# A decoder layer in three stages: staggered stage starts, and a layer norm whose reciprocal root is found by Newton steps on GpSimd

## The chip, the cores and the metric

The kernel runs on one core of a Trainium2 chip. The core has five engines that work side by side, each through its own queue in order: TensorE (PE in the profile, with its weight loads as PEld) for matrix products, VectorE (DVE) for elementwise work, reductions and scans, ScalarE (ACT) for functions taken from tables and for copies, GpSimd (POOL) for further elementwise work, and SyncE (SP), which here issues DMA transfers. Engines wait for each other by semaphores. The metric is the time of one execution on the device in microseconds (us), less being better.

## What is computed

The input `x` has 16 sequences of 256 positions and 256 channels, `ctx_1024` the same shape. Everything is in 32-bit floats. The layer is three blocks, each added to its input and then normalised:

```
x = layernorm(x + mixer(x))
x = layernorm(x + cross_attention(x, ctx, ctx))
x = layernorm(x + feed_forward(x))
layernorm(x) = (x - mean(x)) / sqrt(var(x) + 1e-5)
```

- **mixer**: a projection `x @ in_proj_w`, a causal convolution over four positions, and per head a weight `p_w` (an exponential of a score, times a time weight). Values are multiplied by `theta`; `cos` and `sin` of the products, times a polynomial of the value and `p_w`, are summed cumulatively over positions and divided by the cumulative sum of `p_w`. The result is normalised by its root mean square, projected with `W_re` and `W_im`, gated with a Silu and projected out.
- **cross attention** by autocorrelation: query, key and value projections, a Fourier transform over positions, the correlation of query and key, the five best shifts per head, a softmax over them, and the sum of the values rolled by those shifts.
- **feed-forward**: two branches of eight experts. Each is `(x V) * cumsum(x W)`, weighted by a softmax router with a Gelu layer, and projected back with `U`; the sum goes through `W_O`.

## The kernel before

Sequences are handled in pairs, `NP = 8` pairs in all. Three Python generators emit the instructions of a pair:

- `mixer(p)` (line 407) issues the loads of `x` for pair p+1 (`load_x`, line 86, on SyncE's DMA queue), emits `body(p)` (line 237) and then `front(p + 1)` (line 179). `front` transposes x (L187), projects it (L196, L213), convolves (`convolve`, L172 and L174), and makes the weights, their cumulative sum `den` and the gated products `g` (L222 to L224); its last act is Silu on two tiles (L229). `body` runs four rounds: four DMA transfers spread rows over partitions (`spread`, L235), ScalarE makes the angles and takes sines (L253 to L259), VectorE multiplies and scans (L261, L262, and L117 in `cumsums`), ScalarE squares (L267, L268), TensorE projects and sums (L272, L277). Then comes a square root over `sv` (L289), the output projection (L304) and the layer norm with tag "ml".
- `attention(p)` (line 565) loads the context, transforms and projects (`spectra`: L432, L438, L442, L461, L472, L478), picks the shifts (`choose`, L492 to L526), rolls (`rolled`: L535, L552, L562), and ends with the layer norm "al". `spectra` adds an output bias to `x` on GpSimd (L453).
- `feed_forward(p)` (line 580) transposes x (L589), scans it (L591), runs the router (L599, Gelu at L601, L602, softmax from L611 to L624, L629, L634), broadcasts the router's weights by DMA (L645), runs the two wide products for each of eight blocks (L649, L653) with VectorE's multiplications (L650, L654), then the output product (L663, L664), the layer norm "fl", and writes the result out (L670).

Each generator yields after a piece of work, with a number that stands for its size. `run` (line 313) takes several generators with their totals (70 for a mixer, 45 for an attention, 77 for a feed-forward) and always advances the one that has done the smallest share of its total. So the instructions of the three streams are traced in proportion to each other.

The main loop (line 674) has nine steps. Step p runs `mixer(p)`, `attention(p - 1)` and `feed_forward(p - 2)` together, each from its start to its end; the streams of step p+1 begin to be traced when all of step p are traced. Before it stand `front(0)` and `mixer(0)` with the folding of weights (`fold_weights`, line 365).

The order of tracing is not the order on the engines: a planner takes it as a priority, and places instructions by its own idea of when their inputs and buffers will be ready. It also gives out the buffers. Those that matter here: nine buffers for `x` (half a pair each), `xT` and `fxT` one each, two each for `sn`, `cs` and `ge`, three for `wb`, eight for `e`, and in PSUM two banks for the mixer (`m_bank`) and four that attention and feed-forward share (`f_bank`).

`layernorm` (line 153) works on four tiles of 128x256 at once. VectorE takes mean and variance of each (L158, L159); ScalarE takes the square root of the four variances (L161, with EPS as bias); VectorE makes the reciprocal (L162) and minus mean times reciprocal (L163); ScalarE scales and shifts each tile (L165). ScalarE holds one set of function tables at a time; where the next function is in another set, an ACT_TABLE_LOAD stands before it in the profile, under the line of that function.

Of the kernel before, what the change touches and what calls it, by code (L numbers as in the profile page):

```python
# [11 lines left out]
F32 = mybir.dt.float32  # L12
BF16 = mybir.dt.bfloat16
U32 = mybir.dt.uint32
AF = mybir.ActivationFunctionType
ALU = mybir.AluOpType
# [3 lines left out]
P = 128  # L20
# [9 lines left out]
EPS = 1e-5  # L30
NP = B // 2
HG = 16
MAGIC = 12582912.0
FAR = 3.0e38
TWO_PI = 2.0 * math.pi
TWO_PI_DOWN = float(np.nextafter(np.float32(TWO_PI), np.float32(0.0)))

# [13 lines left out]
def decoder_kernel(ctx: ExitStack, tc: tile.TileContext, a: dict, out: bass.AP):  # L51
    nc = tc.nc
    V, S, G, T = nc.vector, nc.scalar, nc.gpsimd, nc.tensor
# [18 lines left out]
    def m_bank():  # L72
        return m_ps.tile([P, 512], F32, name="mps", tag="mps")
# [4 lines left out]
    def split(ps, n=2):  # L78
        return ps.rearrange("p (c d) -> p c d", c=n)
# [6 lines left out]
    def load_x(b):  # L86
        xs[b] = mx.tile([P, 2, D], F32, name="x", tag="x", bufs=9)
        nc.sync.dma_start(out=xs[b], in_=a["x"][b].rearrange("(c p) d -> p c d", p=P))
# [19 lines left out]
    b_magic, b_half_pi, b_eps = bias_c[:, 0:1], bias_c[:, 1:2], bias_c[:, 2:3]  # L108
# [6 lines left out]
    def cumsums(dst, src):  # L115

        V.tensor_tensor_scan(dst, again[:, : dst.shape[1]], src, 0.0, ALU.mult, ALU.add)  # L117
# [29 lines left out]

    V.tensor_scalar(tcol, tcol, 1.0 / TWO_PI, None, ALU.mult)
    for i in range(2):
# [3 lines left out]
    def layernorm(pool, tag, tiles):  # L153
        n = len(tiles)
        st = pool.tile([P, n, 6], F32, name="ln_st", tag=tag + "st")
        mv = pool.tile([P, n, 2], F32, name="ln_mv", tag=tag + "mv")
        for i, t in enumerate(tiles):
            V.bn_stats(st[:, i, :], t)  # L158
            V.bn_aggr(mv[:, i, :], st[:, i, :])  # L159
        sd = pool.tile([P, 3, n], F32, name="ln_sd", tag=tag + "sd")  # L160
        S.activation(sd[:, 0, :], mv[:, :, 1], AF.Sqrt, bias=b_eps)  # L161
        V.reciprocal(sd[:, 1, :], sd[:, 0, :])  # L162
        V.scalar_tensor_tensor(sd[:, 2, :], mv[:, :, 0], -1.0, sd[:, 1, :], ALU.mult, ALU.mult)  # L163
        for i, t in enumerate(tiles):
            S.activation(t, t, AF.Identity, scale=sd[:, 1, i : i + 1], bias=sd[:, 2, i : i + 1])  # L165


    def convolve(pool, tag, ps, ci, bufs):

        zc = pool.tile([P] + list(ps.shape[1:]), F32, name=tag, tag=tag, bufs=bufs)  # L170
        cw = pv[:, C_CW + 4 * ci : C_CW + 4 * ci + 4]
        S.activation(zc, ps, AF.Identity, bias=pv[:, C_CB + ci : C_CB + ci + 1], scale=cw[:, 3:4])  # L172
        for s in (1, 2, 3):
            V.scalar_tensor_tensor(  # L174
                zc[..., s:], ps[..., : L - s], cw[:, 3 - s : 4 - s], zc[..., s:], ALU.mult, ALU.add
            )
        return zc

    def front(p, made):

        xT = mx.tile([P, 2, 2, L], F32, name="xT", tag="xT")
        for j in range(2):
            ps = m_bank()
            for db in range(2):
                for c in range(2):
                    lo = db * L + c * P
                    T.transpose(ps[:, lo : lo + P], xs[2 * p + j][:, c, db * P : (db + 1) * P], ident)  # L187
            S.copy(xT[:, :, j, :], split(ps))


        ps = m_bank()
        for c in range(2):
            for par in range(2):
                for j in range(2):
                    q = 32 * (2 * par + j)
                    T.matmul(ps[q : q + 32, :L], w_sc[:, c, par, :], xT[:, c, j, :], start=c == 0, stop=c == 1)  # L196
        yield 3
        sc = convolve(mx, "sc", ps[:, :L], 4, 1)
        V.tensor_scalar(sc, sc, pv[:, C_SCALE : C_SCALE + 1], 20.0, ALU.mult, ALU.min)
        V.tensor_scalar(sc, sc, -20.0, None, ALU.max)  # L200
        pw = sc
        S.activation(pw, sc, AF.Exp)
        V.tensor_tensor(pw, pw, tw, ALU.mult)
        den = mx.tile([P, L], F32, name="den", tag="den", bufs=2)
        cumsums(den, pw)
        V.tensor_scalar(den, den, 1e-4, None, ALU.max)
        yield 3

        zcs, gs = [], []
        for m in range(4):  # L210
            ps = m_bank()
            for c in range(2):
                T.matmul(ps, w_in[:, c, m * P : (m + 1) * P], xT[:, c, :, :], start=c == 0, stop=c == 1)  # L213
            zcs.append(convolve(mx, "zc", split(ps), m, 6))
            if m < 2:
                g = mx.tile([P, 2, L], F32, name="g", tag="g", bufs=3)
                ps = m_bank()
                for j in range(2):
                    T.matmul(
                        ps[:, j * L : (j + 1) * L], sel_h[:, j, m * P : (m + 1) * P], pw, start=True, stop=True  # L220
                    )
                S.activation(g, zcs[m], AF.Identity, bias=dw[:, 1:2], scale=dw[:, 3:4])  # L222
                G.tensor_tensor(g, g, zcs[m], ALU.mult)
                V.scalar_tensor_tensor(g, g, dw[:, 0:1], split(ps), ALU.add, ALU.mult)  # L224
                gs.append(g)
            if m < 3:
                yield 4
        for m in (2, 3):
            S.activation(zcs[m], zcs[m], AF.Silu)  # L229
        made[p] = zcs, gs, den  # L230
        yield 4
# [5 lines left out]
    def body(p, made):  # L237
        zcs, gs, den = made.pop(p)
        ss = y_ps.tile([P, L], F32, name="ss", tag="ss")
        for m in range(2):  # L240
            y = y_ps.tile([P, 512], F32, name="y", tag="y")
            for h in range(2):
# [15 lines left out]
                S.activation(cs, cs, AF.Abs)  # L258
                S.activation(cs, cs, AF.Sin, bias=b_half_pi, scale=-TWO_PI)  # L259
                yield 3  # L260
# [38 lines left out]
        for j in range(2):  # L299
# [8 lines left out]
            V.tensor_tensor(x, x, split(ps), ALU.add)  # L308
            tiles += [x[:, 0, :], x[:, 1, :]]
        layernorm(mx, "ml", tiles)  # L310
        yield 4

    def run(*streams):


        left = [[0.0, n, total, gen] for n, (gen, total) in enumerate(streams)]
        while left:
            at = min(left, key=lambda s: (s[0] / s[2], s[1]))
            try:
                at[0] += next(at[3])  # L320
            except StopIteration:
                left.remove(at)

    made = {}
    run((front(0, made), 22))


    f_dft = load("f_dft", [P, 2, 2, 64], eng=G)
# [24 lines left out]
    m5 = const.tile([2 * NH, 8], F32, name="m5", tag="m5")  # L353
    V.memset(m5, FAR)

# [51 lines left out]
    def mixer(p):  # L407
        if 2 * p + 2 < B:
            for b in (2 * p + 2, 2 * p + 3):
                if xs[b] is None:  # L410
                    load_x(b)
        yield from body(p, made)
        if p + 1 < NP:
            yield from front(p + 1, made)

    with tc.tile_pool(name="fold", bufs=1) as fold:
        for b in range(2, 4):
            load_x(b)
        run((mixer(0), 70))
        fold_weights(fold)  # L420

    at = ctx.enter_context(tc.tile_pool(name="at", bufs=1))
# [22 lines left out]
    def load_ctx(b):  # L445
        ct = at.tile([P, 2, D], F32, name="ct", tag="ct", bufs=2)
        nc.sync.dma_start(out=ct, in_=a["ctx"][b].rearrange("(c p) d -> p c d", p=P))
        return ct
# [37 lines left out]
    def choose(prod, wfs):  # L486
# [14 lines left out]
        rest = at.tile([NHP, L], F32, name="rest", tag="rest")  # L501
        V.match_replace(rest, m5, corr, -FAR)
        V.tensor_scalar(m8, m8, top[:, 0:1], None, ALU.add)
# [5 lines left out]
        V.reciprocal(top[:, 4:5], top[:, 3:4])  # L509
        V.scalar_tensor_tensor(corr, rest, -FAR, corr, ALU.is_equal, ALU.mult)  # L510
        S.activation(corr, corr, AF.Identity, scale=top[:, 4:5])
# [53 lines left out]
    def attention(p):  # L565
        prod = at.tile([P, 4, 2 * NH], F32, name="prod", tag="prod", bufs=2)
        pair = (2 * p, 2 * p + 1)
        cts = [load_ctx(b) for b in pair]
        vfs, wfs = [], []
        for b, ct in zip(pair, cts):  # L570
            yield from spectra(b, ct, prod, vfs)
        yield from choose(prod, wfs)
        for b, vf in zip(pair, vfs):
            rolled(b, vf, wfs[0])
            yield 5
        layernorm(at, "al", [xs[b][:, c, :] for b in pair for c in range(2)])
        yield 3
# [93 lines left out]
        yield 3  # L671


    for p in range(1, NP + 2):
        streams = []
        if p < NP:
            streams.append((mixer(p), 70))
        if p - 1 < NP:
            streams.append((attention(p - 1), 45))
        if p >= 2:  # L680
            streams.append((feed_forward(p - 2), 77))
        run(*streams)

# [124 lines left out]
```

## Time and profile before

| What | Value |
|---|---|
| median of 3 runs | 1166.14 us (1166.03 to 1169.14) |
| the profiled execution | 1166.22 us |
| its span on the core | 1164.5 us |
| granted TensorE clock, mean | 0.925 of full speed |
| PE busy | 982.4 us |
| DVE busy | 722.9 us |
| ACT busy | 593.0 us |
| ACT_TABLE_LOAD on ACT | 97, of 1283 ns each |
| POOL busy | 166.3 us |
| layer norms | 24, of four tiles each |

The profile is one execution, taken by the hardware profiler. The span reaches from the first to the last instruction of the core; busy time is the time in which an engine executes instructions. A busy PE is not a PE at its peak: ends of matmuls are modelled, and the granted clock varies. Rows of the form "L163 DVE ..." name a source line, engine, operation and tile. In the table of stretches each row gives start and end, length, then for each engine busy us and number of instructions, then the granted clock, the share of DMA time and GB/s.

### The profile page before, as it was taken

The numbers are of one execution on the slowest core, as the hardware profiler recorded it, in microseconds if no ns is written. First come the engines' busy times: TensorE is split into PE (matmuls) and PEld (weight loads), VectorE is DVE, ScalarE is ACT, GpSimd is POOL, SyncE is SP. The second block draws the span as 40 slices with busy tenths as digits, with TensorE's granted clock in tenths as the row PEclk, the third lists the DMA queues.
The fourth block names the chain that finished last, engine by engine and source line by source line (L and its number), as shares of the span: only waits on it lengthen the run. The fifth ranks groups of instructions, "written<-read, shape, count | busy, mean of one in ns | idle before, by whom it ended". The sixth has DMA issues, their size and how long they took to land.

```text
span 1164.5 us, 10813 instructions
## 1 busy us (share of the span) xinstructions
PE 982.4 (84%) x3820; PEld 542.4 (47%) x3820; DVE 722.9 (62%) x1173; ACT 593.0 (51%) x831; POOL 166.3 (14%) x163
## 2 busy tenths in 40 slices
PE   5878858789987899779987799779988799699787
PEld 2335426234652457334662457334662358246345
DVE  5766877676685666765775766766775754234132
ACT  2865664863288425972279425972279522311310
POOL 4002102020111111210111111211111111101000
PEclk9988869889998899889999899889999899999889
DMA  9612312163043413333033513334032510040050
GB/s 322 158 37 73 81 37 46 36 109 46 2 91 80 82 19 73 82 67 51 1 82 77 95 19 73 73 58 60 1 82 55 89 20 1 18 64 9 19 72 19
DMA packets 45510, 72.04 MB, mean 62 GB/s; under 512 B 4448, under 2 KB 18320, under 8 KB 45456
## 3 DMA queue, kind: packets, MB, share of 16 engines
q1 hardware_dynamic: 44240, 68.04, 29.2%
q0 software_dynamic: 1216, 3.31, 0.9%
q8 instruction: 30, 0.49, 0.2%
q14 instruction: 24, 0.20, 0.0%
HBM read 16.81 MB, written 4.19 MB: 18 GB/s over the span
## 4 chain that ended last, share of the span: by engine, by line
PE 58%; ACT 15%; DVE 14%; DMA 5%; issue 3%; POOL 3%; SPq 1%; POOLq 0%; ACTq 0%; DVEq 0%
PE fps L649 10%; PE fps L653 9%; PE fps L663 5%; PE fps L461 4%; PE fps L599 4%; DMA sn<-zc 3%; PE y L272 3%; DVE cs L117 3%; PE fps L602 2%; PE mps L304 2%; ACT x L165 2%; PE fps L552 2%; PE fps L472 2%; PE mps L213 2%; DVE sn L117 2%
## 5 line engine op out<-in xcount | busy, mean ns | idle before, releaser
L649 PE MATMUL fps<-fcT,w_c 128*128 128x512 f32 x256 | 137.4, 656 | 0.0
L653 PE MATMUL fps<-fxT,w_v 128*128 128x512 f32 x256 | 124.5, 609 | 0.0
L663 PE MATMUL fps<-u_o,e 128*128 128x256 f32 x512 | 116.9, 379 | 0.0
L663 PEld LDWEIGHTS fps<-u_o,e 128*128 128x128 f32 x512 | 97.3, 190 | 15.8 <-issue 2.9
L599 PE MATMUL fps<-fxT,w_h 128*128 128x512 f32 x128 | 75.1, 726 | 15.6 <-ACT fxT L590 15.6
L653 PEld LDWEIGHTS fps<-fxT,w_v 128*128 128x128 f32 x256 | 50.3, 199 | 67.4 <-issue 57.1
L650 DVE TENSOR_TENSOR e<-wb,fps 128x512 f32<-128x512 f32 x64 | 43.7, 683 | 61.0 <-DMA wb<-fwT 31.4
L174 DVE SCALAR_TENSOR_TENSOR zc<-mps,pv,zc 128x510 f32<-128x510 f32 (+2 forms) x96 | 70.7, 738 | 16.1 <-ACT zc L172 15.1
L117 DVE TENSOR_TENSOR_SCAN sn<-again,sn 128x1024 f32<-128x1024 bf16 x32 | 78.0, 2438 | 0.5
L117 DVE TENSOR_TENSOR_SCAN cs<-again,cs 128x1024 f32<-128x1024 bf16 x32 | 77.3, 2415 | 0.4
L213 PE MATMUL mps<-xT,in_proj_w 128*128 128x512 f32 x128 | 65.1, 626 | 13.9 <-DVE g L224 10.2
L261 DVE TENSOR_TENSOR sn<-sn,ge 128x1024 f32<-128x1024 f32 x32 | 43.4, 1356 | 43.7 <-ACT sn L257 36.4
L649 PEld LDWEIGHTS fps<-fcT,w_c 128*128 128x128 f32 x256 | 49.4, 208 | 42.8 <-issue 39.3
L253 ACT ACTIVATE sn<-sn,theta_col 128x512 f32<-128x512 f32 x64 | 45.5, 714 | 46.5 <-DMA sn<-zc 46.0
L654 DVE TENSOR_TENSOR e<-e,fps 128x512 f32<-128x512 f32 x64 | 43.4, 677 | 33.7 <-PE fps L653 32.8
L461 PE MATMUL fps<-Wkv,spec 128*128 128x512 f32 x128 | 61.8, 615 | 2.8 <-ACT spec L442 2.8
L478 POOL TENSOR_TENSOR pp<-qf,kf 128x512 f32<-128x512 f32 x16 | 22.3, 1397 | 278.9 <-ACT qf L476 278.9
L599 PEld LDWEIGHTS fps<-fxT,w_h 128*128 128x128 f32 x128 | 27.3, 231 | 64.6 <-issue 45.3
L272 PE MATMUL y<-cs,w_ri 128*32 128x512 f32 x128 | 38.9, 689 | 20.4 <-DVE cs L117 17.3
L602 PE MATMUL fps<-h,w2t 128*32 128x512 f32 x64 | 34.2, 690 | 25.4 <-ACT h L601 25.4
L165 ACT ACTIVATE x<-x,ln_sd 128x256 f32<-128x256 f32 x96 | 50.1, 588 | 6.6 <-DVE ln_sd L163 6.6
L268 ACT ACTIVATE sq<-cs 128x1024 f32<-128x1024 f32 x32 | 33.7, 1054 | 35.4 <-PE ss L277 29.2
(231 smaller groups left out, 1823.7 us busy)
## 6 DMA issues: line engine op xcount, KB each, us to landing
sn<-zc SPq DMA_DIRECT2D x64, 256.0 KB, 4.7
ge<-g SPq DMA_DIRECT2D x64, 256.0 KB, 4.7
wb<-fwT SPq DMA_DIRECT2D x64, 256.0 KB, 4.4
x<-in_x SPq DMA_DIRECT2D x16, 256.0 KB, 3.1
ct<-in_ctx SPq DMA_DIRECT2D x16, 256.0 KB, 2.7
out<-x SPq DMA_DIRECT2D x16, 256.0 KB, 3.0
in_proj_w<-in_in_proj_w SPq DMA_DIRECT2D x1, 512.0 KB, 6.0
V_fwd<-in_V_fwd SPq DMA_DIRECT2D x1, 512.0 KB, 10.9
```

The costliest lines, as they stand in the source:

```text
L117: V.tensor_tensor_scan(dst, again[:, : dst.shape[1]], src, 0.0, ALU.mult, ALU.add)
L165: S.activation(t, t, AF.Identity, scale=sd[:, 1, i : i + 1], bias=sd[:, 2, i : i + 1])
L174: V.scalar_tensor_tensor(zc[..., s:], ps[..., : L - s], cw[:, 3 - s : 4 - s], zc[..., s:], ALU.mult, ALU.add)
L213: T.matmul(ps, w_in[:, c, m * P : (m + 1) * P], xT[:, c, :, :], start=c == 0, stop=c == 1)
L253: S.activation(sn[:, i, :], sn[:, i, :], AF.Identity, scale=tcol[:, cb : cb + 1])
L272: T.matmul(y[q : q + 32, :], w_ri[:, n, :], part[:, i, :], start=n == 0, stop=n == 1)
L461: T.matmul(ps, cf[:, c, f * P : (f + 1) * P], wkv[:, c, :], start=c == 0, stop=c == 1)
L599: T.matmul(ps, w_h[:, c, br, rb * P : (rb + 1) * P], xT[:, c, :, :], start=c == 0, stop=c == 1)
L602: T.matmul(pl[32 * br : 32 * br + 32, :], w2t[:, rb, :], h, start=rb == 0, stop=rb == 1)
L649: T.matmul(pc, w_c[:, c, br, cut], cT[:, c, :, :], start=c == 0, stop=c == 1)
L653: T.matmul(pv_, w_v[:, c, br, cut], xT[:, c, :, :], start=c == 0, stop=c == 1)
L663: T.matmul(o, es[i][:, cut], u_o[:, i, :], start=i == 0, stop=False)
```

## The change

There are two parts. First, the nine separate runs become one. Every stream gets a start and a length on a common scale of steps: `mixer(p)` starts at p and lasts 1; `attention(p)` starts at p + 1.2 and lasts 1; `feed_forward(p)` starts at p + 2.6 and lasts 1. `run` always advances the stream whose place on that scale is the earliest. Before, the starts in that scale were p, p + 1 and p + 2.

Second, `layernorm` no longer takes a square root on ScalarE. VectorE adds EPS to the variances and makes a first guess of the reciprocal root from the bits of the number (a shift, and a subtraction from a constant); GpSimd improves it in three Newton steps of four operations each, and makes minus mean times the result in two more. All work on 128x4 elements. ScalarE's scaling of the tiles is as before.

```diff
--- before.py
+++ after.py
@@ -32,6 +32,9 @@
 HG = 16
 MAGIC = 12582912.0
 FAR = 3.0e38
+
+A_AT, A_LEN = 0.2, 1.0
+F_AT, F_LEN = 1.6, 1.0
 TWO_PI = 2.0 * math.pi
 TWO_PI_DOWN = float(np.nextafter(np.float32(TWO_PI), np.float32(0.0)))
 
@@ -157,12 +160,21 @@
         for i, t in enumerate(tiles):
             V.bn_stats(st[:, i, :], t)
             V.bn_aggr(mv[:, i, :], st[:, i, :])
-        sd = pool.tile([P, 3, n], F32, name="ln_sd", tag=tag + "sd")
-        S.activation(sd[:, 0, :], mv[:, :, 1], AF.Sqrt, bias=b_eps)
-        V.reciprocal(sd[:, 1, :], sd[:, 0, :])
-        V.scalar_tensor_tensor(sd[:, 2, :], mv[:, :, 0], -1.0, sd[:, 1, :], ALU.mult, ALU.mult)
+
+        rs = pool.tile([P, 5, n], F32, name="ln_rs", tag=tag + "rs")
+        var, y, t, nb, half = (rs[:, i, :] for i in range(5))
+        V.tensor_scalar(var, mv[:, :, 1], EPS, None, ALU.add)
+        V.tensor_scalar(half.bitcast(U32), var.bitcast(U32), 1, None, ALU.logical_shift_right)
+        V.tensor_scalar(y.bitcast(U32), half.bitcast(U32), -1.0, float(0x5F3759DF), ALU.mult, ALU.add)
+        for _ in range(3):
+            G.tensor_tensor(t, y, y, ALU.mult)
+            G.tensor_tensor(t, t, var, ALU.mult)
+            G.tensor_scalar(t, t, -0.5, 1.5, ALU.mult, ALU.add)
+            G.tensor_tensor(y, y, t, ALU.mult)
+        G.tensor_tensor(nb, mv[:, :, 0], y, ALU.mult)
+        G.tensor_scalar(nb, nb, -1.0, None, ALU.mult)
         for i, t in enumerate(tiles):
-            S.activation(t, t, AF.Identity, scale=sd[:, 1, i : i + 1], bias=sd[:, 2, i : i + 1])
+            S.activation(t, t, AF.Identity, scale=y[:, i : i + 1], bias=nb[:, i : i + 1])
 
 
     def convolve(pool, tag, ps, ci, bufs):
@@ -313,16 +325,16 @@
     def run(*streams):
 
 
-        left = [[0.0, n, total, gen] for n, (gen, total) in enumerate(streams)]
+        left = [[start, length / total, gen] for start, length, total, gen in streams]
         while left:
-            at = min(left, key=lambda s: (s[0] / s[2], s[1]))
+            at = min(left, key=lambda s: s[0])
             try:
-                at[0] += next(at[3])
+                at[0] += at[1] * next(at[2])
             except StopIteration:
                 left.remove(at)
 
     made = {}
-    run((front(0, made), 22))
+    run((0, 1, 22, front(0, made)))
 
 
     f_dft = load("f_dft", [P, 2, 2, 64], eng=G)
@@ -416,7 +428,7 @@
     with tc.tile_pool(name="fold", bufs=1) as fold:
         for b in range(2, 4):
             load_x(b)
-        run((mixer(0), 70))
+        run((0, 1, 70, mixer(0)))
         fold_weights(fold)
 
     at = ctx.enter_context(tc.tile_pool(name="at", bufs=1))
@@ -671,15 +683,10 @@
         yield 3
 
 
-    for p in range(1, NP + 2):
-        streams = []
-        if p < NP:
-            streams.append((mixer(p), 70))
-        if p - 1 < NP:
-            streams.append((attention(p - 1), 45))
-        if p >= 2:
-            streams.append((feed_forward(p - 2), 77))
-        run(*streams)
+    streams = [(p, 1.0, 70, mixer(p)) for p in range(1, NP)]
+    streams += [(p + 1 + A_AT, A_LEN, 45, attention(p)) for p in range(NP)]
+    streams += [(p + 1 + F_AT, F_LEN, 77, feed_forward(p)) for p in range(NP)]
+    run(*streams)
 
 
 
```

## The prediction

> **What bounds the kernel now.** I read the first part of the page, then the busy times by stage of the run, then one steady step in slices, then ScalarE's order of time where a slice is poor.
>
> ```profile
> span 1164.5 us, 10813 instructions
> PE 982.4 (84%) x3820; PEld 542.4 (47%) x3820; DVE 722.9 (62%) x1173; ACT 593.0 (51%) x831; POOL 166.3 (14%) x163
> ```
>
> TensorE is the fullest engine, but 16% of the span is without it. Busy time by stage (columns: stretch, its length, then busy us and instructions of PE, PEld, DVE, ACT, POOL, then granted clock, DMA share, GB/s):
>
> ```profile
> 0.00:100.00 100.00, 74.10 (x296) 36.69 (x297) 61.58 (x97) 57.52 (x86) 16.30 (x29) 0.93 0.51 150
> 100.00:203.00 103.00, 77.10 (x326) 43.67 (x324) 78.80 (x123) 60.41 (x86) 23.66 (x23) 0.80 0.29 64
> 335.00:467.00 132.00, 114.79 (x462) 63.76 (x461) 88.43 (x143) 74.36 (x102) 19.85 (x17) 0.94 0.31 60
> 990.00:1086.00 96.00, 84.27 (x282) 48.38 (x280) 34.38 (x77) 20.78 (x41) 9.02 (x10) 0.95 0.18 28
> 1086.00:1164.50 78.50, 61.12 (x168) 31.61 (x168) 19.01 (x42) 12.97 (x21) 0.61 (x1) 0.88 0.23 40
> ```
>
> The run is 100 us (mixer 0, weight folding), 103 us (mixer 1, attention 0), five steps of 132 and one of 127 with all three stages, 96 us (attention 7, feed-forward 6) and 78.5 us (feed-forward 7 alone): together 1164.5. A steady step in slices of 6.6 us shows where it loses:
>
> ```profile
> 350.80:357.40 6.60, 3.24 (x10) 0.83 (x10) 0.61 (x2) 6.54 (x10) 1.48 (x1) 0.77 0.74 204
> 357.40:364.00 6.60, 6.60 (x14) 2.30 (x12) 6.53 (x4) 6.29 (x8) 0.00 (x0) 0.71 0.08 29
> 377.40:384.00 6.60, 1.58 (x5) 1.25 (x6) 6.50 (x9) 4.00 (x5) 1.47 (x1) 0.57 0.53 110
> 443.80:450.40 6.60, 6.60 (x31) 5.42 (x30) 3.99 (x12) 0.78 (x1) 0.00 (x0) 1.00 0.00 0
> ```
>
> In the first slices of the step ScalarE is full and TensorE starves at a low clock; late in the step TensorE is full and ScalarE nearly idle. ScalarE there, in order of time:
>
> ```profile
> 346.83 1.28 ACT L161 ACT_TABLE_LOAD   x1
> 348.91 1.28 ACT L229 ACT_TABLE_LOAD   x1
> 352.82 1.28 ACT L601 ACT_TABLE_LOAD   x1
> 354.82 1.28 ACT L257 ACT_TABLE_LOAD   x1
> ```
>
> These belong to attention's layer norm (square root), the gate's Silu, feed-forward's Gelu and the mixer's sine: all three stages begin together, each with its serial part, and ScalarE changes tables between them. I count 14 loads in the step from 335 to 467; over the run 97, at 1.28 us 124 of its 593 busy us. The chain of waits runs through this knot: attention's normalisation at 350.83, a table load, Gelu, and only then matmuls. So a steady step is bound by TensorE for four fifths and by the common start of the stages for the rest.
>
> **What the Trainium skill says.** ScalarE: Activation LUTs, section "What ACT_TABLE_LOAD costs", gives about 1283 ns for a load plus about 1380 ns of drain; the trace agrees on the load (1283 ns each) and has no row for a drain. TensorE: Matmul & The Clock Gate, section "What's actually happening", says that the array clock falls to half after an idle window and returns after some 3.4 us of work; the trace agrees in direction (0.57 granted in the slice with 1.58 us of matmul, 1.00 in the full one). SBUF — State Buffer, section "Who interferes with whom", says that GpSimd and a VectorE instruction with two SBUF inputs lock each other out of a shared port for a whole instruction; the trace fits it: the 128x512 addition at L453 on GpSimd takes 1266 ns at the least and 3261 at the most.
>
> **The change, part by part.**
>
> 1. *Offsets.* No instruction is added or removed by them. A steady step (the interval between two mixer starts, X) holds the same work. Matmul time at full clock per stage, from the back-to-back rows (0.43 us for 512 columns, 0.216 for 256, packed groups counted once): mixer 23, attention 23, feed-forward 55, so 101 of 132 us. What moves, with each yield's place in the step: the sine blocks lie at 0 to 0.57, Gelu at 0.67 to 0.78, the three groups of exponentials at 0.69 to 0.81, Silu at 0.94; the wide matmuls of feed-forward at 0.83 to 1.6, that is under the sine blocks of the next mixer. Attention ends at 2.2 and feed-forward begins at 2.6, so the norm that held the first Gelu back gets 0.4 of a step of slack.
> What can be won: in the step from 350.8 to 482.8 TensorE is busy 116.8 us, idle 15.2. Its busy time at reduced clock (slices at 0.77, 0.71, 0.57, 0.66, 0.74) loses, share by share, 0.7 + 1.9 + 0.7 + 2.2 + 1.6 = 7 us. So 22 us is the most, and X falls to 110 at best. I take two thirds, 15 us, X = 117. Not all: the mixer's own chain (DMA spread, sine, scans, squares) needed 103 us in the step where only attention 0 competed, VectorE has 88 us of work, and small waits stay.
>
> 2. *Fill and drain.* Feed-forward p starts 0.6 later, so the tail is longer. Up to 200: as now (100 + 100, a fifth of attention 0 goes out). Mixer 2 with attention 1 and 0.4 of feed-forward 0: the 103 us of its like, plus 4 for a start whose 18 us of matmuls fit mostly into gaps (77 busy of 103): 107. Then four full intervals and one with mixer 7, which has no next front, 5 less, as 127 against 132 now. Drain after that: 46/77 of feed-forward 5 (34 us of matmuls), the rest of attention 6 (5) and attention 7 (23) at clock 0.95: 65. Feed-forward 6 and 7 alone cost 78.5 each now; a router start (1084 to 1111, TensorE half empty) can run under the last product of the one before (16 us), as far as the single transposed-x buffer allows: 65 and 72. Sum 202. Span = 100 + 100 + 107 + 4X + (X - 5) + 202 = 504 + 5X. With X = 117: 1089.
>
> 3. *Norm.* Out go 24 square roots on ScalarE (7.1 us), their 13 table loads (16.7), 24 reciprocals and 24 VectorE products (7.9); with the loads that restored another table, and the ordering of part 1, I expect some 7 loads fewer a step. In come three VectorE operations on 128x4 (about 0.16 each by L163, 0.5 a norm) and 14 dependent GpSimd operations on 128x4. The trace has none of that size. Low end: 0.10 each, as the 128x1 memsets (99 ns), 1.4 us. High end: each waits for one VectorE instruction, 2.0 us by L453's spread, 28 us. I take 4 us. The old path took 0.30 + 0.18 + 0.16 plus 13/24 of a load, about 1.3. So a norm grows by 3 us (between +0.6 and +27); no gain in its latency is open. Where it is hidden: mixer norm to attention has 0.57 of a step, attention norm to feed-forward 0.49, both over 50 us. If a normalisation stands early in ScalarE's queue, the evacuations behind it wait for GpSimd, and with them TensorE's banks; with 24 norms x 3 us = 72 us of ScalarE waiting at worst, 9 a step against the 9 us of table loads that leave, I put it at nothing. On GpSimd 42 operations a step wait ahead of the gate product (L223) and attention's products; the engine is 14% busy. At the end of the run the last two norms are bare: +3 each, inside the 72 above.
>
> 4. *Ring of x.* Nine buffers stay. A pair lives from the start of mixer p-1 to the end of feed-forward p: 4.6 steps x 2 = 9.2 tiles, now 8. The second load of mixer p waits for the write-out of feed-forward p-3, issued at p + 0.56, and the transposes that need it come at p + 0.69: 0.125 X = 15 us, for norm and scaling (4 + 2), write-out (3.0) and load (3.1), so 3 us to spare. The load would then stand on SP's queue behind the write-out, with the spreads (L235) and the broadcasts of router weights (L645) behind it; today seven such waits cost 8.9 us in all.
>
> Sum: span 1089; the profiled execution took 1166.22 for a span of 1164.5, so 1.7 more: 1091. Its own time stands 0.1 over the median of the three runs (1166.14), which needs no correction.
>
> **Rivals.**
>
> *The bubbles mostly move.* The instruction order is planned from priorities, not from these offsets alone: already now the `sv` product of the next body (L287) runs at 313, well before its place in the program. A third of the 22 us comes back: X = 125, span 1129, time 1131. For it: the offset starts still have two serial chains each.
>
> *The offsets do nothing.* The planner evens out both orders alike; X = 131, and the longer tail takes the rest: 504 + 655 + 2 = 1161. Up to 1170 this is no difference. Against it: the knot at 340 to 390 recurs in every step.
>
> *Slower: the ring of x meets the slow norm.* Where feed-forward's end to x loaded takes over 15 us, each us more holds up the next front, the mixer and SP's queue. It decides from X = 132 on, since 504 + 5 x 132 + 2 = 1166: that is a norm of about 22 us against my 4, near the high end. With the high end, 28 us, the front waits 21 us, X = 138 and the time is 1196. For it: 9.2 tiles in nine buffers, and VectorE full in many slices. Against it: two inputs in SBUF are held by only part of VectorE's work.
>
> **How the numbers follow.** Forecast (X from 110 to 122, time 1056 to 1116): 0.60, at 1091. Bubbles move (to 1160): 0.18. No difference: 0.06. Slower: 0.16. This measurement can tell 0.3%, 3.5 us, from nothing. Faster is the sum of the first two, 0.78. The range from 1050 to 1180 leaves out some 0.05 below (a shorter drain than 202) and 0.10 above, where the high end of the norm lies.
>
> **What would show it.** Right: the slices of a steady step all have TensorE over 5.5 of 6.6 us and a clock near 1.00; table loads fall from 97 to about 50; attention's normalisation no longer precedes the first Gelu on the chain; distance between two mixers near 117. Wrong: x loads waiting for write-outs and transposes (L187) waiting for them; ScalarE idle ahead of the normalisation, released by GpSimd, for more than 70 us; steady distance at 130 or more, or a drain much over 202.

## The result and the profile after

| | before | after |
|---|---|---|
| median | 1167.64 us (4 runs) | 1151.02 us (4 runs, 1144.82 to 1158.08) |
| ratio to before | 1 | 0.9851, 95% interval 0.9815 to 0.9888 |
| span of the profiled execution | 1164.5 us | 1143.0 us |
| first pair written out at | 351.8 us | 377.6 us |
| from one pair's write-out to the next, mean of pairs 0 to 4 (a steady step) | 132.2 us | 125.4 us |
| from the write-out of pair 4 to the end | 283.7 us | 264.0 us |
| table loads on ScalarE | 97 | 44 |

The kernel became 1.5% faster, where 6.5% was forecast. The profiled execution of the changed kernel was the fastest of its four (1144.82 us). The step times here and below are distances between the first write-out DMAs of successive pairs (L670 before, L682 after). The three parts of the span add up: 377.6 + 4 x 125.4 + 264.0 = 1143. Against before, the first pair comes out 26 us later, four steps save 27 us, and the end saves 20.

The first part of the page of the changed kernel, to be laid beside that of before:

```profile
span 1143.0 us, 11089 instructions
PE 971.6 (85%) x3820; PEld 543.0 (48%) x3820; DVE 718.1 (63%) x1197; ACT 520.8 (46%) x754; POOL 235.1 (21%) x499
```

ScalarE lost 72 us of work and GpSimd won 69. TensorE does the same work in a little less busy time, at a mean granted clock of 0.944 against 0.925; that the clock is the reason is not shown, since the offsets alone, below, need 970.3 us at 0.921. Slices of one steady step of the changed kernel (start and end, length, busy us and instructions of PE, PEld, DVE, ACT, POOL, then granted clock, DMA share, GB/s):

```profile
502.40:508.70 6.30, 3.51 (x17) 2.37 (x15) 3.26 (x4) 6.21 (x10) 1.14 (x2) 1.00 0.44 131
508.70:515.00 6.30, 3.88 (x16) 2.49 (x15) 4.69 (x4) 0.78 (x2) 2.80 (x2) 1.00 0.11 38
521.20:527.50 6.30, 4.77 (x12) 1.40 (x11) 0.76 (x2) 3.23 (x6) 2.98 (x10) 1.00 0.00 0
533.80:540.10 6.30, 3.63 (x11) 2.30 (x11) 6.28 (x21) 4.44 (x8) 1.23 (x1) 0.71 0.13 16
615.40:621.60 6.20, 6.20 (x29) 5.26 (x28) 0.93 (x4) 0.00 (x0) 0.00 (x0) 1.00 0.15 42
```

Of the five slices with a reduced clock (0.57 to 0.77) two are left: the one with 0.71 and the next, with 0.74 and TensorE full. But there are new gaps, and the first three lie just behind a norm: feed-forward's, whose GpSimd operations end at 502.4, and the mixer's, where they end at 523.6. The first is the one to look at: just before it, ScalarE stands still. In order of time, ScalarE of the changed kernel, from the scalings of feed-forward's norm on:

```profile
502.44 2.08 ACT L177 ACTIVATE x<-x,ln_rs 128x256 f32<-128x256 f32 x4 [2.69 <-POOL ln_rs L175]
504.54 1.28 ACT L301 ACT_TABLE_LOAD   x1
505.84 0.42 ACT L301 ACTIVATE sv<-sv 128x256 f32<-128x256 f32 x1
506.16 1.06 ACT L602 COPY fxT<-fps 128x512 f32<-128x512 f32 x2
507.10 0.39 ACT L488 COPY qf<-fps 128x256 f32<-128x256 f32 x1
```

The four scalings of feed-forward's norm (L177) wait 2.69 us for the last Newton operation. Behind them in the queue stand the mixer's square root `sv`, the copies `fxT` for the next feed-forward and `qf` for attention: one piece of each stream. None of the three needs this norm. The input of the root is ready at 502.19, when VectorE has finished it:

```profile
501.77 0.42 DVE L300 SCALAR_TENSOR_TENSOR sv<-ss,sv 128x256 f32<-128x256 f32 x1 [0.18 <-PE ss L289]
```

The root begins at 505.84, 3.65 us later: 2.33 us until the scalings are over, and 1.3 us for a table load of its own, which the norm's root used to bring. GpSimd before that, the first two and the last of its 14 operations:

```profile
498.54 0.20 POOL L170 TENSOR_TENSOR ln_rs<-ln_rs 128x4 f32<-128x4 f32 x1 [9.66 <-DVE ln_rs L168]
498.81 0.20 POOL L171 TENSOR_TENSOR ln_rs<-ln_rs 128x4 f32<-128x4 f32 x1
...
502.19 0.22 POOL L175 TENSOR_SCALAR ln_rs<-ln_rs 128x4 f32<-128x4 f32 x1
```

Each takes about 0.20 us, but they start 0.28 apart: 3.9 us for the chain.

Where the trace says what this comes to, the group of the scalings has, among the costliest groups of the changed kernel:

```profile
L177 ACT ACTIVATE x<-x,ln_rs 128x256 f32<-128x256 f32 x96 | 50.0, 592 | 113.6 <-POOL ln_rs L175 113.6
```

Of the 113.6 us of ScalarE waiting, 50.6 lie before the very last norm, where ScalarE has nothing else to do; 63 us over the other 23 norms are 2.7 us each. Before, the same group had 6.6 us in all.

### The profile page after: what moved, and what is told of

Its sections match the earlier page's. It is cut to its first block, busy times and chain, and to the rows that moved or that the text cites. A ratio compares the mean times of both kernels' runs of the same rounds, so it can differ in the third digit from the quotient of the medians.

```text
span 1143.0 us, 11089 instructions
## 1 busy us (share of the span) xinstructions
PE 971.6 (85%) x3820; PEld 543.0 (48%) x3820; DVE 718.1 (63%) x1197; ACT 520.8 (46%) x754; POOL 235.1 (21%) x499
## 4 chain that ended last, share of the span: by engine, by line
PE 49%; DVE 18%; POOL 7%; ACT 7%; issue 6%; DMA 1%; SPq 0%; POOLq 0%; ACTq 0%; DVEq 0%
PE fps L675 10%; PE fps L661 8%; PE fps L665 7%; PE y L284 3%; DVE zc L186 3%; ACT x L177 2%; PE mps L316 2%; DVE cs L120 2%; PE fps L473 2%; PE fps L450 2%; PE ss L289 2%; PE fps L614 2%; PE fps L574 2%; PE fps L611 1%; PE fps L676 1%
## 5 line engine op out<-in xcount | busy, mean ns | idle before, releaser
L661 PE MATMUL fps<-fcT,w_c 128*128 128x512 f32 x256 | 126.2, 617 | 0.0
L170 POOL TENSOR_TENSOR ln_rs<-ln_rs 128x4 f32<-128x4 f32 x72 | 14.4, 199 | 440.9 <-DVE ln_rs L168 437.1
L177 ACT ACTIVATE x<-x,ln_rs 128x256 f32<-128x256 f32 x96 | 50.0, 592 | 113.6 <-POOL ln_rs L175 113.6
L611 PE MATMUL fps<-fxT,w_h 128*128 128x512 f32 x128 | 66.3, 643 | 18.8 <-ACT fxT L602 18.8
L120 DVE TENSOR_TENSOR_SCAN sn<-again,sn 128x1024 f32<-128x1024 bf16 x32 | 73.1, 2285 | 0.5
L490 POOL TENSOR_TENSOR pp<-qf,kf 128x512 f32<-128x512 f32 x16 | 28.2, 1764 | 189.5 <-ACT qf L488 189.5
L279 ACT ACTIVATE ge<-sn 128x1024 f32<-128x1024 f32 x32 | 33.7, 1054 | 71.2 <-DVE sn L120 49.6
L289 PE MATMUL ss<-ge,ones_bd 128*32 128x256 f32 x256 | 47.4, 409 | 19.2 <-ACT ge L279 19.2
L613 ACT ACTIVATE h<-fps,pv 128x512 f32<-128x512 f32 x32 | 21.2, 681 | 79.9 <-PE fps L611 79.9
L284 PE MATMUL y<-cs,w_ri 128*32 128x512 f32 x128 | 43.6, 660 | 12.8 <-DVE cs L120 11.5
```

The costliest lines, as they stand in the source:

```text
L177: S.activation(t, t, AF.Identity, scale=y[:, i : i + 1], bias=nb[:, i : i + 1])
L284: T.matmul(y[q : q + 32, :], w_ri[:, n, :], part[:, i, :], start=n == 0, stop=n == 1)
L289: T.matmul(ss[q : q + 32, :], ones_bd[:, 4 * m + 2 * h + par, :], s[:, par, j * L : (j + 1) * L], start=m == 0 and h == 0 and n == 0, stop ...
L611: T.matmul(ps, w_h[:, c, br, rb * P : (rb + 1) * P], xT[:, c, :, :], start=c == 0, stop=c == 1)
L661: T.matmul(pc, w_c[:, c, br, cut], cT[:, c, :, :], start=c == 0, stop=c == 1)
```

## The experiments

Each kernel was timed beside the kernel before on the same chip; ratios are to it, with 95% intervals. The medians of before lay between 1165.6 and 1169.1 us in these comparisons, so a few us between two experiments say nothing. The theory formed from the trace (A): the offsets do what was forecast of them, and the Newton norm takes most of it back, on the path. Its rival (B): the norm is covered, and the offsets are worth little.

### The two parts, each alone

Offsets alone: the changed kernel with the old `layernorm` put back.

```diff
-        for _ in range(3):
-            G.tensor_tensor(t, y, y, ALU.mult)
...
+        S.activation(sd[:, 0, :], mv[:, :, 1], AF.Sqrt, bias=b_eps)
+        V.reciprocal(sd[:, 1, :], sd[:, 0, :])
+        V.scalar_tensor_tensor(sd[:, 2, :], mv[:, :, 0], -1.0, sd[:, 1, :], ALU.mult, ALU.mult)
```

> The staggered starts with the old layer norm (square root on ScalarE). Theory A, the Newton chain on GpSimd lies on the path twice a step (end of feed-forward, end of mixer; 14 operations 0.28 us apart, 3.9 us each time against 1.3 us for the old way): this kernel is faster than the changed one by 15 to 35 us, so 1115 to 1136 us, although table loads rise again from 44 towards 65. Theory B, the Newton chain is covered or pays for itself in table loads and the offsets alone are worth little: 1150 to 1165 us.

Measured: 1115.02 us, ratio 0.955 (0.951 to 0.9589); a steady step 118.8 us, 72 table loads.

Newton alone: the kernel before, with its nine steps and its `run`, and the new `layernorm`.

```diff
-        S.activation(sd[:, 0, :], mv[:, :, 1], AF.Sqrt, bias=b_eps)
-        V.reciprocal(sd[:, 1, :], sd[:, 0, :])
...
+        for _ in range(3):
+            G.tensor_tensor(t, y, y, ALU.mult)
...
```

> The old nine steps with the Newton layer norm. Theory A: slower than before by 5 to 30 us (1172 to 1197), since attention's norm stands ahead of the first Gelu on the chain. Theory B: equal or faster, 1145 to 1168 us, since table loads of the norm (13, with as many to restore another table) go out at the busiest place of ScalarE.

Measured: 1236.6 us, ratio 1.0583 (1.0547 to 1.0618); a steady step 141.7 us. The 71 us more than before are above what A expected, and far from B.

So the offsets alone give 4.5%, three times what the whole change gives, and the Newton norm costs 36 us in the new order and 71 in the old. One steady step of the offsets alone, as one stretch, under the same stretch of before and of the changed kernel (first before, then the changed kernel, then offsets alone):

```profile
484.90:616.20 131.30, 113.63 (x464) 63.62 (x464) 89.13 (x142) 74.91 (x103) 19.52 (x18) 0.96 0.33 63
```

```profile
503.60:629.10 125.50, 113.59 (x466) 63.97 (x465) 88.42 (x145) 63.06 (x91) 28.15 (x59) 0.97 0.32 63
```

```profile
504.10:623.60 119.50, 113.56 (x468) 66.19 (x466) 85.99 (x142) 69.01 (x99) 17.50 (x17) 0.94 0.34 67
```

TensorE is busy 113.6 us in all three; idle 17.7, 11.9 and 5.9. ScalarE is least busy in the changed kernel and yet that step is longer than with the offsets alone: the 6 us of ScalarE's work that Newton saves in a step (69.0 against 63.1) buy nothing.

What TensorE waited for in the four steady steps (who waited, for whom, us in all, times, longest wait), the two longest waits of before, three of the changed kernel, and the only two of offsets alone:

```profile
PE fps L634 <- POOL lg L629: 29.9, 4, 7.5
PE fps L602 <- ACT h L601: 14.3, 6, 3.4
```

```profile
PE fps L611 <- ACT fxT L602: 11.2, 4, 2.8
PE fps L614 <- ACT h L613: 6.2, 4, 1.5
PE mps L316 <- DVE zc L308: 5.6, 3, 2.4
```

```profile
PE mps L222 <- DVE sc L206: 16.3, 4, 4.1
PE fps L565 <- ACT aT L560: 6.8, 4, 2.0
```

The offsets took away above all the wait of 7.5 us a step for the router's softmax `lg`, whose small VectorE operations stood between the mixer's multiplications and scans (on the chain of waits from 374.7 to 380.8). The Newton norm brought the three rows in the middle: `fxT` and `zc` come behind feed-forward's norm, `h` behind the mixer's. They make 23.0 us in four steps, 5.8 a step, close to the 6.0 by which the idle time differs. The other waits of the changed kernel are not those of offsets alone, but have the same sum (23.5 against 23.1).

### How hard the chain presses

Twice the Newton steps:

```diff
-        for _ in range(3):
+        for _ in range(6):
```

> The changed kernel with six Newton steps in place of three, so 12 more operations on GpSimd, 3.4 us more a norm. Theory A: two norms a step on the path, 16 in the run: 1151 + 16 x 3.4 = 1205 us, at least 1185. Theory B: under 1165 us.

Measured: 1210.9 us, ratio 1.036 (1.0312 to 1.0408), a steady step 133.2 us. The 60 us more against the changed kernel for 12 operations (3.4 us a norm) are more than 16 norms would make in full (54), and 2.5 us over all 24: the length of the norms is on the path. Which norm presses is not told. Feed-forward's eight would make 27 us, and in this kernel the planner put the mixer's root ahead of feed-forward's scalings (it begins 2.5 us after its last sum on TensorE, against 4.1 in the changed kernel); ScalarE stands idle for 7.1 us ahead of the mixer's scalings in each steady step. Next, the changed kernel with all 14 operations on VectorE:

```diff
-            G.tensor_tensor(t, y, y, ALU.mult)
+            V.tensor_tensor(t, y, y, ALU.mult)
...
```

> The changed kernel with the same 14 operations of the norm on VectorE in place of GpSimd. VectorE's rows of that size run about 0.2 us apart, so a norm's chain becomes about 2.8 us against 3.9, at the cost of some 48 us more VectorE work over the run (336 operations of 0.14). Theory A: 5 to 20 us faster than the changed kernel. Theory B: equal or slower by up to 10 us.

Measured: 1138.42 us, ratio 0.9749 (0.9714 to 0.9784): 12.6 us less than the changed kernel, inside A's span, and still 23 us behind the square root. That a shorter chain is the reason is not shown. Only the mixer's scalings begin sooner after the statistics (3.4 us against 4.6); feed-forward's begin later (7.3 against 5.1), and the planner again put the mixer's root ahead of them.

### Which of the three norms

Both forms of `layernorm` in one kernel, chosen by tag, with the offsets:

```diff
...
+    def layernorm(pool, tag, tiles):
+        (layernorm_newton if tag == "al" else layernorm_sqrt)(pool, tag, tiles)
```

(and "fl", and "ml", in the other two kernels.)

> Staggered starts; Newton on GpSimd in attention's norm alone, square root on ScalarE in the other two. Theory A1, a norm's added latency costs where the chain of waits runs through that norm: attention's norm has some 50 us until feed-forward begins and is not on the chain of a steady step, while its square root would fall among the sines and cost two table loads; so 1105 to 1118 us against 1115 with square roots everywhere. Theory A2, every norm costs alike because ScalarE's queue stands still behind GpSimd: a third of the 36 us, 1127 us.

> Newton on GpSimd in feed-forward's norm alone. Theory A1: it stands on the chain in each steady step, 8 norms with 2 us or more each: 1130 to 1140 us. Theory A2: 1127 us.

> Newton on GpSimd in the mixer's norm alone. Theory A1: on the chain as well, and the next front's transposes are behind it on ScalarE: 1130 to 1140 us. Theory A2: 1127 us.

| Newton in | median | ratio (95%) | steady step | against square roots everywhere (1115.02) |
|---|---|---|---|---|
| attention's norm | 1111.46 | 0.9514 (0.9485 to 0.9543) | 118.6 | -3.6 |
| feed-forward's norm | 1151.08 | 0.9852 (0.9825 to 0.988) | 124.7 | +36.1 |
| mixer's norm | 1121.95 | 0.9607 (0.956 to 0.9654) | 120.9 | +6.9 |
| all three (the change) | 1151.02 | 0.9851 (0.9815 to 0.9888) | 125.4 | +36.0 |

Neither theory had it whole. Attention's norm is as A1 said (it costs nothing; whether it gains is not told, the two intervals overlap), the mixer's costs less than expected (and here too the intervals overlap), and feed-forward's alone costs more than expected: as much as all three together. Where feed-forward's result is needed does not explain that, for nothing waits soon for its output but the write-out. The trace points to the place in ScalarE's queue. The same place with square roots (offsets alone, ScalarE in order of time):

```profile
500.71 0.30 ACT L164 ACTIVATE ln_sd<-ln_mv,bias_c 128x4 f32<-128x4 f32 x1 [7.62 <-DVE ln_mv L162]
502.47 0.37 ACT L469 COPY kf<-fps 128x256 f32<-128x256 f32 x1 [1.46 <-PE fps L464]
502.74 0.38 ACT L470 COPY vf<-fps 128x256 f32<-128x256 f32 x1
503.00 2.08 ACT L168 ACTIVATE x<-x,ln_sd 128x256 f32<-128x256 f32 x4
505.59 0.42 ACT L292 ACTIVATE sv<-sv 128x256 f32<-128x256 f32 x1 [0.51 <-DVE sv L291]
505.92 1.05 ACT L593 COPY fxT<-fps 128x512 f32<-128x512 f32 x2
```

Here the scalings find their scale ready and are over before the root's input is; the mixer's root finds its table loaded, since the load for the norm's root had run at 491.81, in ScalarE's idle time. From the statistics (end of L162, at 500.7 here, at 497.3 in the changed kernel) to the copies `fxT` it takes 5.2 us here and 8.9 us there: 3.7 us, where a step is 5.9 us longer with Newton in this norm alone. The mixer's root comes late alike in all five places where feed-forward's norm meets a mixer: 4.1 us after its last sum on TensorE, against 0.5 with square roots. The rest of the 36 us was not followed.

### Taking the wait out of ScalarE's queue

The changed kernel, with feed-forward's scalings put behind the Newton steps on GpSimd:

```diff
         for i, t in enumerate(tiles):
-            S.activation(t, t, AF.Identity, scale=y[:, i : i + 1], bias=nb[:, i : i + 1])
+            if tag == "fl":
+                G.tensor_scalar(t, t, y[:, i : i + 1], nb[:, i : i + 1], ALU.mult, ALU.add)
+            else:
+                S.activation(t, t, AF.Identity, scale=y[:, i : i + 1], bias=nb[:, i : i + 1])
```

> The changed kernel, with one edit: the four scalings of feed-forward's norm run on GpSimd behind its Newton steps, so that ScalarE's queue no longer holds a wait for them; the norm itself is finished later than in the changed kernel (four operations on 128x256 of some 0.4 to 0.7 us in place of 2.1 us). Theory Q, it is ScalarE's queue that made feed-forward's norm cost 36 us (copies for attention and feed-forward and the mixer's root stand behind the scalings): most of it comes back, 1112 to 1130 us. Theory L, it is the lateness of the normalised x itself (write-out, next load of x): no gain or worse, 1148 to 1165 us.

Measured: 1127.53 us, ratio 0.9641 (0.962 to 0.9662), a steady step 122.0. The norm as such is not finished sooner (7.4 us after its statistics, 7.2 in the changed kernel), yet 23.5 of the 36 us come back: theory Q. TensorE's waits for `fxT` fall from 18.8 us in the run to 5.0. The edit takes both the wait and the 2.1 us of the scalings themselves out of ScalarE's queue; the two are not separated. The chain of waits of this kernel past the same place, with the columns start, duration, and what:

```profile
622.59 0.86 PE ss L292 x8
623.45 1.02 PE fps L604 x8
624.48 1.74 PE fps L487 x8
626.31 0.42 DVE qf L490
626.74 1.66 DVE sv L305
628.40 2.24 DVE fcT L120
```

No step of feed-forward's norm stands in it; while GpSimd works on the norm, TensorE goes on. (The mixer's norm, with its 14 operations from 639.40 on, does stand on this chain.)

The same with a square root in the mixer's norm:

```diff
...
+    def layernorm(pool, tag, tiles):
+        (layernorm_newton if tag != "ml" else layernorm_sqrt)(pool, tag, tiles)
```

(with the scalings of "fl" on GpSimd as above.)

> Staggered starts; square root in the mixer's norm, Newton in attention's (scaling on ScalarE) and in feed-forward's (scaling on GpSimd). Theory Q: 1100 to 1115 us, at or under the 1111 us of Newton in attention's norm alone, since feed-forward's root leaves ScalarE too. Theory L: 1130 us or more.

Measured: 1127.11 us, ratio 0.9638 (0.9616 to 0.9659). That is a miss for both: not the 1111 of Newton in attention's norm alone, so feed-forward's norm costs 16 us even when ScalarE's queue is free of it. One suspect is GpSimd's own queue, where attention's product `pp` stands behind some 6 us of norm. The trace speaks against it. In the kernel above, with Newton in all three norms, ScalarE and then GpSimd:

```profile
624.68 1.28 ACT L304 ACT_TABLE_LOAD   x1
625.97 0.42 ACT L304 ACTIVATE sv<-sv 128x256 f32<-128x256 f32 x1
```

```profile
627.23 1.27 POOL L493 TENSOR_TENSOR pp<-qf,kf 128x512 f32<-128x512 f32 x1 [0.82 <-ACT qf L491]
```

GpSimd has been idle for 0.82 us when `pp` begins, and what `pp` waited for is `qf`. The table load of the mixer's root, though, is still there, on the path. It is the same in this kernel: the load, `pp` after 0.82 us of idle time, and the root 2.5 us after its last sum, against 0.5 with Newton in attention's norm alone. In the same stretch TensorE waits 0.7 us for `fxT` and 1.5 for `zc`, where it has none with Newton in attention's norm alone, and a step takes 120.7 us against 118.6. By the spans (1125.5 against 1108.1) the four steps make 8.5 of 17 us; the rest, at the start and the end of the run, was not followed. No kernel without this load was run.

### Where the stages begin

With square roots, feed-forward at 1.4; with square roots, attention at 0 (and feed-forward at 1.6); with Newton in attention's norm alone, feed-forward at 1.8:

```diff
-F_AT, F_LEN = 1.6, 1.0
+F_AT, F_LEN = 1.4, 1.0
```

> Staggered starts with square roots, feed-forward starting at 1.4 in place of 1.6. If a steady step depends on where the serial parts lie and 1.6 is a good place, 118.8 us a step grows by 1 to 4 us and the run is 1115 to 1130 us, although fill and drain are 0.2 of a step shorter. If only some offset matters, the shorter fill and drain show alone: 1095 to 1112 us.

```diff
-A_AT, A_LEN = 0.2, 1.0
+A_AT, A_LEN = 0.0, 1.0
```

> Square roots in all norms; attention starts with the mixer again (offset 0 in place of 0.2), feed-forward stays at 1.6. If it is feed-forward's offset that carries the gain (its Gelu away from the sines, and slack after attention's norm), a steady step stays within 2 us of 118.8: 1105 to 1128 us. If attention's 0.2 is needed as well, a step is 123 us or more and the run 1133 to 1165 us.

```diff
-F_AT, F_LEN = 1.6, 1.0
+F_AT, F_LEN = 1.8, 1.0
```

> Newton in attention's norm alone, feed-forward starting at 1.8 in place of 1.6 (the step with 1.4 was 9.2 us longer). If 1.6 is near the best place, the steady step grows again and the run is 1120 to 1150 us; if what counts is that feed-forward's serial part keeps away from the mixer's sines, a step stays at 118.6 and fill and drain add up to 20 us: 1112 to 1132 us.

| attention, feed-forward start | norm | median | ratio (95%) | steady step |
|---|---|---|---|---|
| 0.2, 1.6 | square roots | 1115.02 | 0.955 (0.951 to 0.9589) | 118.8 |
| 0.2, 1.4 | square roots | 1156.09 | 0.9888 (0.9862 to 0.9915) | 128.0 |
| 0, 1.6 | square roots | 1133.9 | 0.9726 (0.968 to 0.9772) | 124.1 |
| 0.2, 1.6 | Newton in attention's | 1111.46 | 0.9514 (0.9485 to 0.9543) | 118.6 |
| 0.2, 1.8 | Newton in attention's | 1207.02 | 1.033 (1.0301 to 1.036) | 138.2 |

Both offsets are needed, and the place is narrow: 0.2 of a step to either side of feed-forward's start loses 41 us and 96 us. Both of these runs are slower than either expectation had it, so the reasons that were written down do not suffice; attention at 0 came out as expected of a kernel that needs both. For 1.8 the trace shows a reason: the ring of nine x buffers, which the prediction had named as a rival for 1.6. In order of time, SyncE, the norm and the transposes of the next mixer:

```profile
541.96 0.57 PEld L217 LDWEIGHTS mps<-ident,x 128*128 128x128 f32 x4
554.15 2.07 ACT L168 ACTIVATE x<-x,ln_sd 128x256 f32<-128x256 f32 x4 [0.55 <-DVE ln_sd L166]
555.27 1.36 SPq L700 DMA_DIRECT2D out<-x  x2
557.43 1.40 SPq L91 DMA_DIRECT2D x<-in_x  x2
560.10 0.50 PEld L217 LDWEIGHTS mps<-ident,x 128*128 128x128 f32 x4 [1.16 <-DMA x<-in_x]
```

The first half of the pair is transposed at 542, the second can't be until feed-forward of an earlier pair has ended and been written out: 18 us, while a step is 19.6 us longer. In each of the last four pairs these transposes follow the issue of the load by 2.6 to 3.0 us, as soon as it has landed. No kernel with more than nine buffers was run, so how much of the 96 us this makes is not shown. In the changed kernel the ring is not felt:

```profile
377.58 1.36 SPq L682 DMA_DIRECT2D out<-x  x2
379.80 1.30 SPq L91 DMA_DIRECT2D x<-in_x  x2
401.31 0.74 PEld L199 LDWEIGHTS mps<-ident,x 128*128 128x128 f32 x7 [0.84 <-issue]
```

The loads are issued 21.5 us before the transposes of the pair. Why 1.4 is worse than 1.6 by 9 us a step stays open.

## Why the prediction was wrong

- **What bounds the kernel; the knot of the stage starts.** Right in the place: with the offsets alone the knot dissolves, and TensorE's idle time in a step falls from 17.7 to 5.9 us. But the prediction looked at ScalarE and its table loads, and the longest of TensorE's waits there, 7.5 us a step, was for the router's softmax on VectorE and GpSimd.
- **Offsets: 15 of 22 us a step, X = 117.** Right: 118.8 with offsets alone. Of the 22 us, 13 came back (132.2 to 118.8), and all of it as idle time; the low clock that was to go as well did not in that kernel (0.94 after 0.96 in the stretches above).
- **Fill and drain: 504 + 5X.** Roughly. With offsets alone, the first write-out is at 384.2 where the working gives 100 + 100 + 107 + 0.56 x 117 = 372.5, and the rest after pair 4 is 251.1 where it gives 1089 - 372.5 - 468 = 248.5. That is 11.7 and 2.6 us too little, and 7.1 more for four steps of 118.8, 21 in all: the span is 1110.3 for the forecast 1089.
- **Norm: "I put it at nothing".** This is the step that failed. The sizes were right: 3.9 us for the chain where 4 was taken, 63 us of ScalarE's waiting where 72 "at worst" was worked out, 44 table loads where about 50 was forecast. The wrong step was to set the waiting off against ScalarE's saved work. ScalarE was 46% busy; its saved work bought nothing, while the wait at the head of its queue held up what stood behind. The table loads did not pay either: 25 of the 53 that left went with the offsets (97 to 72), 28 with the norm (72 to 44), and the load for feed-forward's root, which had run in ScalarE's idle time, gave way to one on the path, for the mixer's root. The norm cost 36 us by the medians, and 33 by the spans (1143.0 against 1110.3), of the 54 us between the forecast span and the measured one; the rest is the 21 us above.
- **Where the norm is hidden.** Attention's: right, it costs nothing that can be told. The mixer's: alone 7 us, which the intervals do not separate from nothing; in the changed kernel TensorE waits 1.5 us a step for `h` behind it. Feed-forward's was not asked about except in the drain. What its wait delays is not its result but pieces of all three streams behind it in ScalarE's queue. The prediction had the sentence ("the evacuations behind it wait for GpSimd, and with them TensorE's banks") and then cancelled it.
- **Rivals.** "The bubbles mostly move", with X = 125 and 1131 us, has the measured step (125.4), but for another reason than it gave: the offsets did not fall short, the norm took the gain back. "The offsets do nothing" fell by the offsets alone. The ring of x did not show at 1.6, where loads landed some 19 us before their transposes and 3 us to spare had been worked out; it did at 1.8, and there with a square root in feed-forward's norm.
- **The lock between GpSimd and VectorE.** The range from 0.6 to 27 us a norm was right to be wide. In the changed kernel the 14 operations ran undisturbed, 0.28 us apart, and none took more than 0.37. In the old order they did not, see below.

## What to carry to other kernels

An operation moved off an engine that is not the bound may give back nothing by its own time, as here; look for what stands behind the moved operation's consumer in its queue, for all streams, and price the new wait there, and the table load that the operation used to bring for the next one. A chain of 14 tiny dependent operations on GpSimd, 3.9 us, in place of one table function cost 36 us in the one norm behind which other streams stood in ScalarE's queue, and nothing that can be told in the norm whose stream had slack: so choose the form per place. Here offsets with a square root in two norms and Newton in attention's gave 1111.46 us, ratio 0.9514 (0.9485 to 0.9543), better than both kernels; and when streams are staggered, try the neighbouring offsets, since 0.2 of a step was worth up to 96 us.

## What the runs showed of the hardware

The time of small GpSimd operations is not in proportion to their elements: 128x4 takes 0.20 us, where the 128x512 addition of the output bias takes 1.27 at the least, and dependent ones start 0.28 us apart. And they can be shut out for long: in the old order with Newton alone, GpSimd in order of time

```profile
502.26 3.24 POOL L167 TENSOR_TENSOR ln_rs<-ln_rs 128x4 f32<-128x4 f32 x1 [8.04 <-DVE ln_rs L165]
505.58 2.10 POOL L168 TENSOR_TENSOR ln_rs<-ln_rs 128x4 f32<-128x4 f32 x1
507.77 0.29 POOL L169 TENSOR_SCALAR ln_rs<-ln_rs 128x4 f32<-128x4 f32 x1
```

and VectorE at the same time:

```profile
502.09 1.22 DVE L271 TENSOR_TENSOR cs<-cs,ge 128x1024 f32<-128x1024 f32 x1
503.23 2.28 DVE L117 TENSOR_TENSOR_SCAN sn<-again,sn 128x1024 f32<-128x1024 bf16 x1
505.43 2.27 DVE L117 TENSOR_TENSOR_SCAN cs<-again,cs 128x1024 f32<-128x1024 bf16 x1
```

Two GpSimd operations of 0.2 us end at 505.50 and 507.68, just as VectorE's scans end (505.51 and 507.70): it looks as if they waited out whole VectorE instructions with two inputs in SBUF, 5 us for one norm. This fits the Trainium skill, SBUF — State Buffer, section "Who interferes with whom", by which a VectorE instruction with two SBUF inputs contends with a GpSimd instruction that reads SBUF, under an exclusive lock. The norms' GpSimd operations took 99.7 us in that run, against 67.5 in the changed kernel. How much of the 71 us of that kernel is this, and how much the chain itself, was not separated.
